# Turning the rows of 36 time steps by DMA over 16-bit planes instead of on TensorE, and loading the first weight block in quarters

## The chip, the core and the metric

One core of a Trainium2 chip runs the whole program. It has five engines that each work through their own instructions in order: TensorE (PE, with its weight load PEld), VectorE (DVE), ScalarE (ACT), GpSimd (POOL) and SyncE (SP, which only issues transfers here). An instruction that waits for a semaphore holds everything behind it on its engine. The metric is the device time of one execution in microseconds (us), lower is better.

## What is computed

The input `x` is 128 rows (b) x 64 time steps (t) x 512 values, so 8192 tokens. A GRU (hidden size 512) runs over the 64 steps; its output goes through a linear layer with ternary weights and is added to `x`. Then a causal convolution along b and a mixture of experts follow, whose sum with `x` is the output. Cut to what matters here:

```
x = x + ffn0(gru(cond_2048, x))            # 64 steps, one after the other
c = conv(x, cond_2048)                     # tokens that the second half works on
y = moe(c): softmax(c @ gate_w.T), top 6 of 64 experts, SwiGLU of each (512 -> 352 -> 512)
shared = silu(c @ sw_gate) * (c @ sw_up) @ sw_down        # 512 -> 704 -> 512, all tokens
out = x + y + shared
```

All matrix products are 32-bit floats.

## The kernel before

The program has four stages, and TensorE is at work in all of them: the GRU (0 to about 1150 us), the convolution (to about 1280 us), the shared experts with the routing (to about 1765 us), and the routed experts, with the rest of the shared ones between them (to the end).

**The first stage's start.** `load_xt(0, ...)` brings the first step's input, and `load_halves` (L295) each input weight block of 1 MB in two transfers of 512 KB, all on SP's queue. TensorE multiplies the raw weights at once (`products`, L336), and DVE and ACT cut each 128 x 512 part into a high, a low and a mixed part (`convert`, L356 to L366).

**The convolution's result** lies in two tiles, `hid0` and `hid1`, of 128 partitions (b) x 32 steps x 512 values; `hid(t)` is one step's 128 x 512 values (2 KB in each partition, 256 KB in all).

**The third stage** has 16 groups of NB = 4 steps; `rows_of(i)` are the steps 4i to 4i + 3. The loop over `i` in 0..7 does in each iteration:

- `shared(i)`: the shared experts of group i. Five blocks (`Block`) of seven products each (`winograd`, L824: two fp32 products of 256 columns), then two times seven for the way back (`Down`). Products 1, 6, 7, 3 (of the block before), 2, 4, 5 write into the PSUM banks `psx`, `y`, `psw`, `psz`. Product 1 is copied out of `psx` by ACT (L853), product 2 is then added onto the same bank, and ACT's silu (L864) reads it; only after that may the next block's product 1 write `psx`. DVE does the sums (L855, L858, L867, L860, L861, L870, L871). `shared` is a generator: it yields 44 times.
- `route` of the groups 2i + 1 and 2i + 2, some pieces of it at each yield of `shared`. Each of their 8 steps has to be turned first, so that the 512 values lie across partitions: `turn(t)` (L1120) makes four TensorE transposes of 128 x 128 (L1128) into a PSUM bank, and DVE copies the bank back over `hid(t)` (L1138). For steps from 32 on the turned rows are also stored to `xts` in HBM by SP (L1144), since a later stage reads them. Then come the gate products (`lg`, L1152), softmax, top 6 and counts; SP stores the scores (L1196).
- `add_shared(i)`: POOL issues four transfers that add group i's result, which stands in `rows_of(i)` by then, to the output in HBM (L1106).

Iteration i also uses `rows_of(i - 2)` as scratch space for its sums (`sums_space`), from i = 2 on. Before the loop `put_rows` stores the unturned rows to `tab`, all through SP's queue.

The order on each engine is set by a scheduler that takes the instructions in the order written, but moves an instruction forward where its own estimate says that the engine would be free and the operands ready. What stands in an engine's list is then done strictly in that order.

Of the kernel before, what the change touches and what calls it, by code (L numbers as in the profile page):

```python
# [9 lines left out]
BF16 = mybir.dt.bfloat16  # L10
I32 = mybir.dt.int32
U8 = mybir.dt.uint8
F32R = mybir.dt.float32r
AF = mybir.ActivationFunctionType
ALU = mybir.AluOpType
# [4 lines left out]
P = 128  # L20
B = 128
T = 64
D = 512
KD = D // P
# [23 lines left out]
def adaln_ffn_kernel(  # L48
# [22 lines left out]
    nc = tc.nc  # L71
# [10 lines left out]
    xts = dram.tile([T // 2, P, D], F32, name="xts")  # L82
# [10 lines left out]
        out=before,  # L93
        in_=before,
# [11 lines left out]
    def load_rows(dst, src):  # L106

        return nc.sync.dma_start(out=dst, in_=src.rearrange("(k p) n -> p k n", p=P))
# [98 lines left out]
    HK = KD // 2  # L207
    HD = D // 2
    gis_ = ExitStack()
    ps_gi = gis_.enter_context(tc.tile_pool(name="ps_gi", bufs=1, space=PSUM))  # L210
    with (
# [19 lines left out]
        def planes(pool, name):  # L231
            return [pool.tile([P, KD, D], F32R, name=f"{name}{n}") for n in "hls"]

# [7 lines left out]
        raw_i = [st.tile([P, KD, D], F32, name=f"rawi{c}") for c in range(3)]  # L241
# [9 lines left out]
        cols = [slice(c * D, (c + 1) * D) for c in range(3)]  # L251
        xps, xns, parts_of = {}, {}, {}

        def load_xt(t, queue=nc.gpsimd):
            xps[t] = xpp.tile([P, KD, B], F32, name="xp")
            queue.dma_start(out=xps[t], in_=xT[t])
# [34 lines left out]
        def repeated(dst, row):  # L291
            nc.sync.dma_start(out=dst, in_=row.partition_broadcast(P))

        def load_halves(dst, src):
            for k in range(2):  # L295
                load_rows(dst[:, k * HK : (k + 1) * HK], src[k * HD : (k + 1) * HD])

        h = el0.tile([P, D], F32, name="h")
        bh = {0: io0.tile([P, D], F32, name="xn"), 1: el0.tile([P, D], F32, name="n")}

        load_xt(0, nc.sync)
        load_halves(raw_i[0], w_ih[:, cols[0]])
        load_halves(raw_i[2], w_ih[:, cols[2]])
        nc.sync.dma_start(out=h, in_=cond)
        load_xt(1, nc.sync)
        load_halves(raw_i[1], w_ih[:, cols[1]])
        load_rows(raw_h[0], w_hh[:, cols[0]])
        repeated(br, b_ih[cols[0]])
        repeated(bh[0], b_hh[cols[0]])
# [20 lines left out]
        def banks(c):  # L330
            pool = ps_gh if c == 1 else ps_gi
            return [pool.tile([P, D], F32, name=n) for n in BANKS[c]]
# [37 lines left out]
        def split_x(t):  # L370

            xp = xps.pop(t)
            cut = xpp.tile([P, KD, B], F32, name="xcut", bufs=1)
            parts_of[t] = [el0.tile([P, KD, B], F32R, name=f"x{n}") for n in "hls"]
            xh, xl, xs = parts_of[t]
# [46 lines left out]
        def place(t, n):  # L422

            if t < T - TAIL:
                return xpp.tile([P, KD, B], F32R, name=f"h{n}", bufs=1)
            return el0.tile([P, KD, B], F32R, name=f"x{n}")

# [52 lines left out]
        def cell_r(t, ps):  # L480
            a, b = ps
            r = el0.tile([P, D], F32, name="rz")
            if t == 0:
                nc.vector.tensor_add(r, b, br)
            else:
                nc.vector.scalar_tensor_tensor(r, a, WHOLE, br, ALU.mult, ALU.add)
                nc.vector.tensor_add(r, b, r)  # L487
            nc.scalar.activation(r, r, AF.Sigmoid)  # L488
            return r

        def cell_n(t, ps, r):
            a, b = ps
            n = el0.tile([P, D], F32, name="n")
            if a is None:
                nc.vector.tensor_add(n, b, bhn)
            else:
                nc.vector.scalar_tensor_tensor(n, a, WHOLE, bhn, ALU.mult, ALU.add)
                nc.vector.tensor_add(n, b, n)
            nc.vector.tensor_mul(n, n, r)
            nc.vector.tensor_add(n, n, gis.pop((t, 2)))  # L500
            nc.scalar.activation(n, n, AF.Tanh)  # L501
            nc.vector.tensor_sub(h, h, n)
            return n
# [15 lines left out]
        for c in (0, 2, 1):  # L519
            a, b = banks(c)  # L520
# [14 lines left out]
        r = cell_r(0, first[0])  # L535
        n = cell_n(0, (None, first[2][1]), r)
# [41 lines left out]
        for t in range(1, T):  # L578
# [17 lines left out]
            r = cell_r(t, ps_r)  # L596
            n = cell_n(t, ps_n, r)
# [11 lines left out]
            if t in (1, 2):  # L609
# [9 lines left out]
                else:  # L619
                    sgn = wh0.enter_context(  # L620
                        tc.tile_pool(name="sgn", bufs=1, reuse_waits="tile")
                    ).tile([P, KD, D], F32R, name="sgn")
                    wf = wi.tile([P, KD, D], F32, name="q")
# [37 lines left out]
    TH = T // 2  # L661


    cum = ctx.enter_context(tc.tile_pool(name="cum", bufs=1)).tile([P, T, NE], U8, name="cum")
    first = ExitStack()
# [9 lines left out]
    def hid(t):  # L675
        return hids[t // TH][:, t % TH, :]
# [21 lines left out]
    with tc.tile_pool(name="ps_c", bufs=4, space=PSUM) as ps_c:  # L698
        for sl in range(NSL):
# [6 lines left out]
            for g in range(DS // 4):  # L706
# [4 lines left out]
                d = slice(g * 4, g * 4 + 4)  # L711
# [9 lines left out]
            if sl >= TAIL_AT:  # L721
# [3 lines left out]
                d = slice(0 if sl == TAIL_AT else 2 * DS * sl, 2 * DS * (sl + 1))  # L725
# [3 lines left out]
            for n in range(2):  # L729
                if sl == NSL - 2 + n:  # L730
                    d = slice(2 * DS * sl, 2 * DS * (sl + 1))
# [61 lines left out]
    NB = 4  # L793
# [3 lines left out]
    def behind(instructions, when=True):  # L797
        return tc.issue_after(instructions[-1].ins) if when and instructions else nullcontext()
    NI = T // NB
# [304 lines left out]
    def add_shared(i):  # L1104
        for t in range(i * NB, i * NB + NB):
            nc.gpsimd.dma_start(out=out_t[t], in_=rows_of(i)[:, t % NB], accum_op=ALU.add)  # L1106


    with (
# [10 lines left out]
        def turn(t):  # L1120

            if t in (2, 3):
                ps = ps_y.tile([P, D], F32, name="y")
            else:
                ps = ps_t1.tile([P, D], F32, name="pst1")
            ps = ps.rearrange("p (k b) -> p k b", k=KD)
            for k in range(KD):
                last = nc.tensor.transpose(ps[:, k, :], hid(t)[:, k * P : (k + 1) * P], ident)  # L1128
            return ps, last

        def route(its, turned={}):


            for i in its:
                for t in range(i * NB, i * NB + NB):
                    ps = turned[t] if t in turned else turn(t)[0]
                    with behind(marks, t in turned):
                        copied = nc.vector.tensor_copy(  # L1138
                            hid(t).rearrange("p (k b) -> p k b", k=KD), ps
                        )  # L1140
                    if t == NB - 1:
                        marks.append(copied)
                    if t >= TH:
                        nc.sync.dma_start(out=xts[t - TH], in_=hid(t))  # L1144
                    yield
# [21 lines left out]
            for n, i in enumerate(its):  # L1167
# [27 lines left out]
                for a in range(2):  # L1195
                    nc.sync.dma_start(  # L1196
                        out=tab_t[i * NB + 2 * a : i * NB + 2 * a + 2, :, D:].rearrange(
                            "t b e -> b t e"
                        ),
                        in_=sc[:, a::2, :NE],  # L1200
# [7 lines left out]
                for j in range(NB):  # L1208
                    t, r = i * NB + j, 2 * (j % 2) + j // 2
# [17 lines left out]
        def put_rows(i):  # L1227
            if i < NI:

                with tc.issue_after(loaded.ins):  # L1230
                    for t in range(i * NB, i * NB + NB):
                        (nc.gpsimd if i == 1 else nc.sync).dma_start(
                            out=tab_t[t, :, :D], in_=hid(t)
                        )
# [5 lines left out]
        for j in range(2):  # L1240
            nc.sync.dma_start(out=swdr[j * rest : (j + 1) * rest, :], in_=sw_down[full * P :, :])

        ahead = route([0])
        for _ in range(NB):
            next(ahead)
# [8 lines left out]
        for i in range(NI // 2):  # L1254
            put_rows(2 * i + 3)
            put_rows(2 * i + 4)

            def routing():
                if i == 0:
                    yield from ahead  # L1260
                its = [r for r in (2 * i + 1, 2 * i + 2) if r < NI]
                yield from route(its, second if i == 0 else {})

            routing_ = routing()
            done = 0
            for n, _ in enumerate(shared(i)):
                if done * PIECES <= n * 20:
                    with behind(products or marks, i == 0):
                        next(routing_, None)
                    done += 1  # L1270
            for _ in routing_:
                pass
            add_shared(i)
    first.close()
# [324 lines left out]
    for i in range(NI // 2 + 1, NI):  # L1599
        n = i - NI // 2 - 1  # L1600
        sums = None
        if i == NI - 1:
# [3 lines left out]
                out=sums, in_=out_t[i * NB : (i + 1) * NB].rearrange("t b d -> b t d")  # L1606
# [58 lines left out]
```

## Time and profile before

| | us |
|---|---|
| three runs | 2452.25, 2450.68, 2452.76 (median 2452.25) |
| the profiled execution: its own time | 2452.42 |
| its span, first to last instruction | 2450.7 |
| one iteration of the third stage's loop (i = 2 to 6) | 59.5 |
| DVE / ACT / POOL busy in one such iteration (i = 3) | 37.6 / 14.4 / 3.5 |

The profile is of one execution. A chain of waits follows the work that ended last back to the start; a group's row gives how often an instruction ran and for how long; a timeline row gives start, duration, engine, line and, in brackets, how long the engine was idle before and what ended that. Matmuls overlap, so their durations in a timeline add up to more than the time they take; the chain gives the time that each adds. The granted TensorE clock is 0.999 of full speed over the span.

### The profile page before, as it was taken

What the parts mean: (1) busy time and instruction counts of PE and PEld (TensorE: products, weight loads), DVE (VectorE), ACT (ScalarE), POOL (GpSimd) and SP (SyncE); (2) the same over time, 40 slices, a digit from 0 to 9 for tenths busy, and PEclk for the clock granted to TensorE, in tenths of its full rate; (3) what the DMA queues carried; (4) which work ended last, traced back from release to release, by engine and by line L of the source; (5) the groups of instructions that cost most, each with busy time, mean ns of one, the idle gap of its engine ahead of it and who ended that gap; (6) DMA issues with size and microseconds to landing.
All of it is one profiled execution on the core that took longest, in us unless ns stands there. A gap on an engine that the chain in (4) does not pass through costs nothing.

```text
span 2450.7 us, 32124 instructions
## 1 busy us (share of the span) xinstructions
PE 2436.9 (99%) x12317; PEld 1883.7 (77%) x12317; DVE 1546.5 (63%) x3073; ACT 463.1 (19%) x847; POOL 445.8 (18%) x468
## 2 busy tenths in 40 slices
PE   9999999999999999999999999999999999999999
PEld 5888888888888888888896688888876666666667
DVE  8877777777777776777686566666653433343344
ACT  5211111111111111111122222222211111111111
POOL 1122221122112112211220000000012222222220
PEclk9999999999999999999999999999999999999999
DMA  5244443333232223222497112222468999899962
GB/s 183 68 95 81 82 80 63 61 69 65 56 61 56 56 56 62 56 52 52 142 343 270 24 23 44 62 59 61 116 174 287 300 290 312 267 330 293 283 175 52
DMA packets 464456, 322.33 MB, mean 132 GB/s; under 512 B 316592, under 2 KB 384176, under 8 KB 462128
## 3 DMA queue, kind: packets, MB, share of 16 engines
q1 hardware_dynamic: 435408, 246.34, 35.6%
q0 software_dynamic: 28896, 73.95, 13.5%
q8 instruction: 97, 1.59, 0.3%
q14 instruction: 55, 0.45, 0.1%
HBM read 233.44 MB, written 92.03 MB: 133 GB/s over the span
## 4 chain that ended last, share of the span: by engine, by line
PE 98%; DMA 1%; DVE 0%; issue 0%; ACT 0%; SPq 0%; POOL 0%; DVEq 0%; ACTq 0%
PE psa L336 9%; PE psx L336 9%; PE psw L336 9%; PE psx L824 8%; PE psw L824 8%; PE psz L824 8%; PE psy L336 5%; PE psb L336 5%; PE psz L336 5%; PE psf L336 5%; PE y L824 4%; PE py L1550 3%; PE pg L1524 3%; PE pu L1524 3%; PE y L1001 2%; PE psc L193 2%
## 5 line engine op out<-in xcount | busy, mean ns | idle before, releaser
L1534 DVE SCALAR_TENSOR_TENSOR a<-a,rw,pu 128x352 f32<-128x352 f32 x32 | 18.6, 580 | 213.4 <-PE pu L1524 213.4
L354 DVE SCALAR_TENSOR_TENSOR xs<-xl,xcut 128x512 fp32r<-128x512 f32 x63 | 103.6, 1644 | 66.0 <-POOL xl L353 66.0
L347 DVE TENSOR_SCALAR hcut<-pst 128x512 int32<-128x512 int32 x63 | 43.5, 691 | 129.8 <-PE pst L419 127.6
L1106 POOL DMA_DIRECT2D out_dram<-hid x32 | 27.7, 1006 | 449.6 <-issue 333.5
L353 POOL TENSOR_TENSOR xl<-xp,xcut 128x512 fp32r<-128x512 f32 x60 | 82.8, 1380 | 145.2 <-PE psa L336 145.1
L488 ACT ACTIVATE rz<-rz 128x512 f32<-128x512 f32 x64 | 40.5, 633 | 336.1 <-DVE rz L487 336.1
L433 ACT CAST hh<-hcut 128x512 fp32r<-128x512 f32 x61 | 37.9, 622 | 325.0 <-DVE hcut L347 325.0
L271 POOL DMA_DIRECT2D q<-in_x_dram x36 | 19.3, 537 | 409.7 <-DMA out_dram<-q 313.4
L1550 PE MATMUL py<-wd,aeT 128*64 128x512 f32 (+1 forms) x384 | 88.8, 597 | 0.0
L1524 PE MATMUL pg<-wg,xeT 128*64 128x352 f32 x512 | 81.2, 459 | 0.0
L1524 PE MATMUL pu<-wu,xeT 128*64 128x352 f32 x512 | 81.2, 459 | 0.0
L1561 POOL DMA_INDIRECT out_dram<-ys,idxp x32 | 47.0, 1469 | 183.4 <-DMA out_dram<-ys,idxo 103.7
L1561 POOL DMA_INDIRECT out_dram<-ys,idxo x32 | 45.0, 1407 | 174.3 <-DMA out_dram<-ys,idxp 168.1
L336 PE MATMUL psa<-wih1h,xh 128*128 128x512 f32 x252 | 74.5, 416 | 0.0
L271 POOL DMA_DIRECT2D xn<-in_x_dram x28 | 15.0, 536 | 319.1 <-DMA out_dram<-xn 258.3
L1524 PEld LDWEIGHTS pg<-wg,xeT 128*64 128x64 f32 x512 | 36.3, 136 | 47.4 <-issue 47.4
L864 ACT ACTIVATE g<-psx 128x256 f32<-128x256 f32 x80 | 30.7, 384 | 217.5 <-DVE aT L871 158.5
L501 ACT ACTIVATE n<-n 128x512 f32<-128x512 f32 x64 | 40.5, 633 | 163.3 <-DVE n L500 160.9
L336 PE MATMUL psw<-wih2h,xh 128*128 128x512 f32 x252 | 68.7, 394 | 0.0
L336 PE MATMUL psw<-wih2l,xl 128*128 128x512 f32 x252 | 68.5, 392 | 0.0
L336 PE MATMUL psa<-wih1l,xl 128*128 128x512 f32 x252 | 68.2, 392 | 0.0
L336 PE MATMUL psb<-wih1s,xs 128*128 128x512 f32 x252 | 68.1, 392 | 0.0
(429 smaller groups left out, 6170.2 us busy)
## 6 DMA issues: line engine op xcount, KB each, us to landing
wg<-in_w_gate_dram SPq DMA_DIRECT2D x64, 704.0 KB, 12.5
wu<-in_w_up_dram SPq DMA_DIRECT2D x64, 704.0 KB, 12.8
wd<-in_w_down_dram SPq DMA_DIRECT2D x64, 512.0 KB, 10.5
xc<-x1c SPq DMA_DIRECT2D x32, 512.0 KB, 6.8
xp<-in_xT_dram POOLq DMA_DIRECT2D x62, 256.0 KB, 2.9
tab<-hid SPq DMA_DIRECT2D x56, 256.0 KB, 4.3
wd<-in_w_down_dram SPq DMA_DIRECT2D x64, 192.0 KB, 10.7
q<-in_x_dram POOLq DMA_DIRECT2D x36, 256.0 KB, 2.9
```

Source lines behind the costliest of these rows:

```text
L193: i = nc.tensor.matmul(ps[rows, j].rearrange("p h (u t) -> p h u t", u=2), xcs[sl % NCB][:, rows, g * 4 + j], tzs[sl % NCB][:, :, :, g * 4 ...
L336: i = nc.tensor.matmul(ps, lhs[:, k, :], rhs[:, k, :], start=start and k == 0, stop=stop and k == KD - 1, skip_group_check=True,)
L347: return nc.vector.tensor_scalar(dst.bitcast(I32), src.bitcast(I32), LOW, None, ALU.bitwise_and)
L353: i = engine.tensor_sub(lo, full, cut)
L354: nc.vector.scalar_tensor_tensor(mix, lo.bitcast(F32), -SPLIT, cut, ALU.mult, ALU.add)
L488: nc.scalar.activation(r, r, AF.Sigmoid)
L501: nc.scalar.activation(n, n, AF.Tanh)
L824: i = nc.tensor.matmul(ps.rearrange("p (j b) -> p j b", b=P) if len(r.shape) == 3 else ps, lhs(k), r, start=(first and k == 0), stop=(k == ...
L1001: nc.tensor.matmul(gu.rearrange("p (j b) -> p j b", b=P), swr[:, k].rearrange("p w n -> p (w n)"), rows[:, k], start=(k == 0), stop=(k == ...
L1524: nc.tensor.matmul(acc[halves[j]], self.xeT[:, k, halves[j]], self.ws[j][which][:, k, :], start=(k == 0), stop=(k == KD - 1),)
L1550: nc.tensor.matmul(py[halves[j]], self.aeT[:n, c, halves[j]], self.ws[j][2][:n, c, :], start=(c == 0), stop=(c == len(ech) - 1),)
L1561: nc.gpsimd.indirect_dma_start(out=out, out_offset=bass.IndirectOffsetOnAxis(ap=(idxp[:CAP] if j == 0 else idxo)[:, q : q + 1], axis=0), i ...
```

## The change

Two edits, both in how data is moved:

1. Steps from 28 on (groups 7 to 15, 36 steps) are no longer turned on TensorE. `turn_away(i)`, run beside iteration i from i = 2 on, turns the groups 2i + 3 and 2i + 4, which are routed in iteration i + 1. For each step ACT copies the low and the high 16-bit halves of the 512 words into two planes of 512 half-words (`flat_at`, two buffers in turn), one SP transfer turns the 128 x 1024 half-words (`dma_start_transpose`, into `turned_at`, three buffers in turn), and two steps later DVE copies the two turned planes back as the halves of the words of `hid(t)`. The buffers are rows of `hid` that are done with: for i = 2 the rows 4, 5 and 6, 7, 3; after that 0, 1 and 2, 3, 7. `route` leaves out its turning loop, with its eight yields, from i = 3 on.
2. At the start the first input weight block comes in four transfers of 256 KB instead of two of 512 KB, and the first step's input is issued by ACT instead of SP. The other blocks stay in halves.

```diff
-        def load_halves(dst, src):
-            for k in range(2):
-                load_rows(dst[:, k * HK : (k + 1) * HK], src[k * HD : (k + 1) * HD])
+        def load_parts(dst, src, n=2):
+            for k in range(n):
+                load_rows(
+                    dst[:, k * KD // n : (k + 1) * KD // n], src[k * D // n : (k + 1) * D // n]
+                )
...
-        load_xt(0, nc.sync)
-        load_halves(raw_i[0], w_ih[:, cols[0]])
+        load_xt(0, nc.scalar)
+        load_parts(raw_i[0], w_ih[:, cols[0]], KD)
...
+        AWAY = 2
+        LAG = 2
+        def plane(t, n):
+            return hid(t).bitcast(U16)[:, n * D : (n + 1) * D]
+        def word_halves(t):
+            return hid(t).bitcast(U16).rearrange("p (d h) -> p d h", h=2)
+        def turn_away(i):
+            steps = [
+                t for r in (2 * i + 3, 2 * i + 4) if r < NI for t in range(r * NB, r * NB + NB)
+            ]
+            flat_at, turned_at = ((4, 5), (6, 7, 3)) if i == AWAY else ((0, 1), (2, 3, 7))
+            for n in range(len(steps) + LAG if steps else 0):
+                for w in range(2) if n < len(steps) else ():
+                    at = flat_at[n % 2]
+                    nc.scalar.copy(plane(at, w), word_halves(steps[n])[:, :, w])
+                    if w:
+                        nc.sync.dma_start_transpose(
+                            out=hid(turned_at[n % 3]).bitcast(U16).rearrange(
+                                "p (m b) -> p m b", b=P
+                            ),
+                            in_=hid(at).bitcast(U16),
+                        )
+                    yield
+                for w in range(2) if n >= LAG else ():
+                    t, at = steps[n - LAG], turned_at[(n - LAG) % 3]
+                    nc.vector.tensor_copy(word_halves(t)[:, :, w], plane(at, w))
+                    if w and t >= TH:
+                        nc.sync.dma_start(out=xts[t - TH], in_=hid(t))
+                    yield
...
-            for i in its:
+            for i in its if its[0] <= 2 * AWAY + 2 else ():
...
+            turning = turn_away(i) if i >= AWAY else iter(())
             for n, _ in enumerate(shared(i)):
                 if done * PIECES <= n * 20:
                     with behind(products or marks, i == 0):
                         next(routing_, None)
                     done += 1
+                next(turning, None)
             for _ in routing_:
                 pass
+            for _ in turning:
+                pass
             add_shared(i)
```

More of the change, by code (lines that the diff above doesn't have):

```diff
@@ L12 @@
 U8 = mybir.dt.uint8
+U16 = mybir.dt.uint16
 F32R = mybir.dt.float32r
@@ L292, in repeated @@
             nc.sync.dma_start(out=dst, in_=row.partition_broadcast(P))
-        def load_halves(dst, src):
-            for k in range(2):
-                load_rows(dst[:, k * HK : (k + 1) * HK], src[k * HD : (k + 1) * HD])
+        def load_parts(dst, src, n=2):
[3 more added lines that the diff above has]
+                )
         h = el0.tile([P, D], F32, name="h")
         bh = {0: io0.tile([P, D], F32, name="xn"), 1: el0.tile([P, D], F32, name="n")}
-        load_xt(0, nc.sync)
-        load_halves(raw_i[0], w_ih[:, cols[0]])
-        load_halves(raw_i[2], w_ih[:, cols[2]])
+        load_xt(0, nc.scalar)
+        load_parts(raw_i[0], w_ih[:, cols[0]], KD)
+        load_parts(raw_i[2], w_ih[:, cols[2]])
         nc.sync.dma_start(out=h, in_=cond)
         load_xt(1, nc.sync)
-        load_halves(raw_i[1], w_ih[:, cols[1]])
+        load_parts(raw_i[1], w_ih[:, cols[1]])
         load_rows(raw_h[0], w_hh[:, cols[0]])
```

## The prediction

> **What bounds the kernel now.** I first read the page's engine shares and the chain of work that ended last.
>
> ```profile
> PE 2436.9 (99%) x12317; PEld 1883.7 (77%) x12317; DVE 1546.5 (63%) x3073; ACT 463.1 (19%) x847; POOL 445.8 (18%) x468
> ...
> PE 98%; DMA 1%; DVE 0%; issue 0%; ACT 0%; SPq 0%; POOL 0%; DVEq 0%; ACTq 0%
> ```
>
> TensorE sets the end nearly everywhere, so work taken from it counts in full, as long as nothing else makes it wait. Next the chain in order of time, inside iteration 3 of the third stage:
>
> ```profile
> 1473.35 0.86 PE psw L824 x4
> 1474.21 0.44 PE pst L1128 x4
> 1474.65 0.86 PE psx L824 x4
> ...
> 1482.01 0.86 PE psx L824 x4
> 1482.88 0.44 PE pst L1128 x4
> 1483.31 0.86 PE psw L824 x4
> ```
>
> There is no gap: each product of two 256-column matmuls takes 0.86, and one step's four transposes take 0.44 between them. Busy times of this whole iteration (columns: stretch, length, PE, PEld, DVE, ACT, POOL, clock, share of the DMA engines, GB/s) show room on all other engines:
>
> ```profile
> 1467.55:1527.05 59.50, 59.50 (x306) 48.44 (x305) 37.56 (x114) 14.37 (x28) 3.46 (x4) 1.00 0.21 41
> ```
>
> For transfers I read the 256 KB rows of the same iteration (median us to landing):
>
> ```profile
> out_dram<-hid POOLq DMA_DIRECT2D x5, 256.0 KB, 5.6
> xts<-hid SPq DMA_DIRECT2D x4, 256.0 KB, 2.0
> ```
>
> The first quick one is a plain SP transfer, the other POOL's adding one. Then the timeline around the start of iteration 2, where the change begins:
>
> ```profile
> 1408.96 1.73 POOL L1106 DMA_DIRECT2D out_dram<-hid  x2 [8.11 <-ACT hid L1076]
> ...
> 1416.11 0.38 ACT L864 ACTIVATE g<-psx 128x256 f32<-128x256 f32 x1 [2.72 <-PE psx L824]
> ...
> 1423.55 0.39 ACT L864 ACTIVATE g<-psx 128x256 f32<-128x256 f32 x1 [4.10 <-DVE aT L871]
> ```
>
> Last the start of the kernel:
>
> ```profile
> 1.26 3.99 DMA rawi<-in_w_ih_dram
> ...
> 5.27 0.76 DVE L347 TENSOR_SCALAR cut<-rawi 128x512 int32<-128x512 int32 x2 [4.20 <-DMA rawi<-in_w_ih_dram]
> ```
>
> DVE first waits for half a weight block; from 5.27 to 40.53, when the first state is ready, it is busy 33.6 of 35.3 us, so DVE sets the pace there.
>
> **Transposes off TensorE: -15.7.** 36 steps x 0.435 (0.44 in the chain, 0.43 to 0.44 by the starts). TensorE's other work keeps its order, except that the gate products come earlier in an iteration. Iterations 3 to 6 shrink by 8 x 0.435 = 3.5 to 56.0, and iteration 7 by 1.7. It is worth the whole only if the products then follow without a gap. Already now, where nothing is left to turn (1438 to 1442), they follow at 0.86.
>
> **The start: -0.8.** The first quarter takes the place of the step's input on SP (issue at 0.81 instead of 1.26), and its 256 KB is half of what had to land. A 256 KB transfer in this trace lands after 2.0 at best, so at 2.8 at the earliest; at worst it lands like the half block, 3.99 after 0.81, at 4.8. DVE thus starts 0.45 to 2.4 earlier, but two issues more and one fewer on SP (0.5 each by its 1.97 for four) push the later blocks back 0.5, and the scheduler regroups the conversions. I take 0.8, bounds +1.0 and -1.5.
>
> **The new work by engine, off the path.** ACT: 72 copies of 128 x 512. The nearest row is ACT's 128 x 512 copy (L1076), 0.59. In ACT's list the 72 stand between the end of iteration 1 and the last block of iteration 4, so about 24 per iteration: 24 x 0.59 + 14.4 = 28.6 of 56. DVE: 36 copies out of PSUM go (0.69 each), 72 half-word copies come. None is in the trace; one-input rows are 0.42 (L347, SBUF to SBUF) and 0.69 (L1138). As they write every second half-word I take 0.69: 37.6 - 5.5 + 24 x 0.69 = 48.7 of 56. Both fit, so their throughput costs nothing. That cover is gone when a DVE copy takes 1.0 (37.6 - 5.5 + 24c = 56).
>
> **The turning transfer.** Its time T, from issue to landing, decides the rest. The trace has none. Below: 2.0, the plain 256 KB of the same stage and queue. Above: 5.6, POOL's adding transfer. I take 2.9, next to the slowest of the 32 `xts` stores (3.0) and equal to the input loads of the first stage (2.9).
>
> [...]
>
> **Where T costs.** ACT has two flat buffers: copy pair n + 2 waits for transfer n, and it stands in ACT's list in front of the silus that free `psx`. Two steps thus take T + 1.25 (two copies at 0.6 and a hand-over). In iteration 2 the first turned buffers are rows 6 and 7, which POOL's add of iteration 1 must have read: issued at 1408.96, landed 4.9 later (that stretch's median), at 1413.9. SP holds the first transfer until then. In ACT's list the pairs of steps 30 to 35 stand before block 1's silu L864, which comes at 1423.55 now; block 2's first product starts at 1425.54. After the first transfer the pairs of steps 30, 32, 34 and 35 (1.25 each) and two more transfers follow one another, so the silu would end at 1413.9 + T + (2T + 5.0) + 0.8 (ACT's two own operations in between) + 0.4, so TensorE stalls 3T - 5.4: 0.6 at 2.0, **3.3** at 2.9, 7.5 at 4.3 (median of the crowded `tab` stores), 11.4 at 5.6. The stalls inside block 0 and of DVE, which waits for turned planes ahead of its sums, are contained in this lag rather than added.
>
> The other 28 steps stand in two clusters: nine between 1451.5 and 1475.6 (4.5 cycles, 5.3 each) and seventeen in about 46 us of iterations 3 and 4 (8.5 cycles, 5.4 each). They keep up while T + 1.25 is below 5.35, T below 4.1, and cost 13 us per us above it. SP adds head-of-line waits: score stores (L1196, landing 1.7) stand behind transfers that wait for ACT, and DVE's next softmax writes the same tile. I allow 2 for that and for DVE's waits, from 0 to 6.
>
> **Sum:** -15.7 - 0.8 + 3.3 + 2.0 = -11.2 against the profiled execution's 2452.4 (span 2450.7, 1.7 around it; the median of the runs is 2452.25): **2441.2**. Its own range: 2435.8 (-15.7 - 1.5 + 0.6) to 2448.0 (T = 4.3: -15.7 - 0.8 + 7.5 + 2.6 + 2.0).
>
> **Rivals.**
> - *Given back (same).* T of 4.1 to 4.6 leaves between -5 and 0, about 2450. Or the fourth stage takes the gain: DMA is at 9 tenths in several late slices, streaming expert weights. Against that, the chain has DMA at 1% and its weight loads are released by TensorE, so they move with it; were it so, 2452.
> - *ACT's list becomes the bound (slower).* Place: the copy pairs that wait for a turning transfer ahead of `psx`'s silus, iterations 2 to 4. Price at T = 5.6: 11.4 + 13 x 1.5 + 2.0 - 16.5 = +16.4, so 2469. It loses from T = 4.6 on (3T - 5.4 + 13(T - 4.1) + 2 = 16.5). For it: large transfers at the start land after 10, the adding one after up to 10.9, and no row shows a transfer that scatters half-words. Against: DMA engines are at 0.21 here.
> - *DVE becomes the bound (slower).* If a half-word copy takes 1.38, twice the PSUM row, DVE needs 37.6 - 5.5 + 33.1 = 65.2 per iteration against 56, three times +9.2: -11.2 + 27.6 = +16.4, 2469. It loses above about 1.14. For it: the first stage's L354 takes 1.64 on average for 128 x 512, and the profile doesn't say why. Against: all other full-size rows of DVE lie between 0.42 and 0.95.
>
> **Chances.** Forecast 0.56, given back 0.17, ACT's list 0.17, DVE 0.10. A difference under 0.2% (4.9 us; the three runs spread over 2.1) I call the same. Faster 0.56, same 0.17, slower 0.27. The range goes from 2435.5, the forecast's low end, to 2461, halfway into the slower cases, and leaves out about 0.2 of the chance.
>
> **What would show it.** 36 of the 64 steps are gone from the L1128 group, and iterations 5 and 6, with no turning left beside them, last 56.0. Iteration 2 lasts about 63 instead of 59.5, TensorE idle before `psx` behind ACT's silu, ACT idle before half-word copies behind the turning transfer. Transfers land near 2.9, DVE half-word copies take 0.42 to 0.69. The first DVE conversion starts near 4.4. Wrong would be: T above 4.6, iterations 3 and 4 longer than 59.5, half-word copies above 1.1, or a gap in the experts' stage that eats the 11 us.

## The result: slower by 8 us

The changed kernel takes 2460.1 us (median of 8 runs, 2458.1 to 2461.3) against 2451.8 for the kernel before (8 runs beside it, 2450.7 to 2452.8): ratio 1.0033, interval 1.0022 to 1.0044. Forecast was 2441.2. The profiled execution took 2460.3 with a span of 2458.6, 7.9 more than before.

The page's engine line and chain shares of the changed kernel:

```profile
PE 2430.6 (99%) x12173; PEld 1875.5 (76%) x12173; DVE 1545.1 (63%) x3109; ACT 501.7 (20%) x919; POOL 448.2 (18%) x468
...
PE 39%; DMA 2%; ACT 1%; DVE 0%; issue 0%; SPq 0%; DVEq 0%; ACTq 0%
```

The shares of the second line cover only the span from 1406.6 on: followed back from the end, the chain stops there, at an adding transfer of POOL. Over the whole span little shows: TensorE is still at 99%, with 144 matmuls less (36 steps of 4), and 6 us less busy though 15.7 us of work were taken off. That gap says that the remaining products ran slower somewhere. The stretches of iterations 2 to 5 of the third stage show where (columns: stretch, length, PE, PEld, DVE, ACT, POOL, clock, share of the DMA engines, GB/s):

```profile
1405.10:1471.70 66.60, 62.76 (x306) 50.30 (x304) 41.86 (x130) 26.04 (x49) 3.46 (x4) 0.95 0.44 87
1471.70:1537.60 65.90, 60.57 (x274) 47.34 (x272) 39.59 (x126) 24.57 (x48) 3.46 (x4) 0.92 0.46 92
1537.60:1603.80 66.20, 61.02 (x275) 46.83 (x273) 42.79 (x139) 29.68 (x58) 3.46 (x4) 0.95 0.70 152
1603.80:1659.80 56.00, 56.00 (x275) 45.42 (x273) 32.62 (x106) 14.45 (x29) 3.46 (x4) 1.00 0.16 24
```

All 36 turnings lie in the first three rows. Iteration 5, with none beside it, takes the 56.0 that all should. Iteration 2, which still turns eight steps on TensorE, has 59.5 us of work, iterations 3 and 4 have 56.0. So 27.2 us are lost: 14.35 with TensorE idle (length less PE) and 12.85 with it busy longer than its work, at a clock of 0.92 to 0.95. In these rows DVE has over 23 us to spare and ACT over 36: neither is short of throughput.

The chain in order of time passes from iteration 2 into iteration 3 without a product of TensorE for over 30 us:

```profile
1466.44 5.77 DMA hid<-hid
...
1472.23 1.14 ACT hid L1154 x2
1473.36 0.28 ACT hid L975
1473.64 1.13 SPq L1156
...
1474.87 7.64 DMA hid<-hid
...
1482.53 0.47 DVE hid L1165
...
1483.06 0.61 ACT hid L1154
...
1483.69 3.04 DMA hid<-hid
...
1486.83 0.47 DVE hid L1165
...
1487.34 0.61 ACT hid L1154
1487.95 0.26 ACT g L1200
1488.21 3.52 DMA hid<-hid
...
1491.81 0.62 ACT hid L1154
1492.43 0.28 ACT g L867
```

`DMA hid<-hid` is the turning transfer, L1154 ACT's copies into planes, L1165 DVE's copies back. Transfer, copy, transfer, copy follow one another, and what TensorE needs (the logits' copy L1200, the silu L867) stands behind them in ACT's list. POOL issues the adding transfers of iteration 2 in two pairs:

```profile
1464.56 1.73 POOL L1109 DMA_DIRECT2D out_dram<-hid  x2 [56.73 <-ACT u L924]
1474.19 1.73 POOL L1109 DMA_DIRECT2D out_dram<-hid  x2 [7.90 <-ACT hid L975]
```

These pairs land after 5.3 and 7.1 in the median. The two turning transfers that run beside them take 5.77 and 7.64, the later ones 3.04 and 3.52. What TensorE does at the start of iteration 2 and in this stretch (its timeline, in brackets the idle time before and what ended it), and two stretches of the clock:

```profile
1416.54 2.07 PE L827 MATMUL psw<-hid,st 128*128 128x256 f32 x4 [3.38 <-DVE u L861]
...
1479.92 1.03 PE L827 MATMUL y<-hid,st 128*128 128x256 f32 x4
1483.61 2.08 PE L827 MATMUL psw<-hid,sw1first 128*128 128x256 f32 x4 [2.67 <-DVE hid L1026]
1488.27 0.69 PE L1213 MATMUL pst<-ident,g 128*128 128x128 f32 x2 [2.58 <-ACT g L1200]
```

```profile
1485.00:1490.00 5.00, 2.42 (x7) 1.50 (x6) 1.66 (x5) 2.52 (x6) 0.00 (x0) 0.50 1.07 272
...
1495.00:1500.00 5.00, 5.00 (x25) 4.41 (x24) 4.82 (x27) 3.62 (x7) 0.00 (x0) 1.00 0.49 140
```

In iteration 2 it waits for DVE's sum L861, in iteration 3 first for DVE's sum L1026, which stands behind a half-word copy, then for ACT's copy L1200; between and after the waits products take up to 2.08 instead of 1.03, with the clock at 0.53 from 1415 to 1420 and at 0.50 from 1485 to 1490.

Over the run, the groups and issue rows (after the last bar: idle before, and what ended it):

```profile
L1154 ACT COPY hid<-hid 128x512 uint16<-128x512 uint16 x72 | 42.0, 616 | 58.7 <-DMA hid<-hid 53.3 <-DMA out_dram<-hid 4.8 <-PE y L827 0.4
...
L1165 DVE COPY hid<-hid 128x512 uint16<-128x512 uint16 x72 | 30.7, 452 | 35.1 <-DMA hid<-hid 35.0
```

```profile
hid<-hid SPq DMA_TRANSPOSE x36, 3.2
```

The transfers land after 3.0 at the least, 3.2 in the median, 7.6 at most. At the start DVE's first conversion comes at 4.75 instead of 5.27 and the third stage begins at 1282.1 instead of 1285.0.

### The profile page after: what moved, and what is told of

The parts are those of the page before. It is cut to its first block, busy times and chain, and to the rows that moved or that the text cites. A ratio compares the mean times of both kernels' runs of the same rounds, so it can differ in the third digit from the quotient of the medians.

```text
span 2458.6 us, 32041 instructions
## 1 busy us (share of the span) xinstructions
PE 2430.6 (99%) x12173; PEld 1875.5 (76%) x12173; DVE 1545.1 (63%) x3109; ACT 501.7 (20%) x919; POOL 448.2 (18%) x468
## 5 line engine op out<-in xcount | busy, mean ns | idle before, releaser
L350 DVE TENSOR_SCALAR hcut<-pst 128x512 int32<-128x512 int32 x63 | 43.5, 691 | 130.6 <-PE pst L422 128.4
L858 DVE TENSOR_TENSOR u<-u,y 128x256 f32<-128x256 f32 x80 | 33.5, 419 | 60.8 <-PE y L827 56.1
L867 ACT ACTIVATE g<-psx 128x256 f32<-128x256 f32 x80 | 30.6, 383 | 200.1 <-DVE aT L874 152.2
L339 PE MATMUL psy<-wih0s,xs 128*128 128x512 f32 x252 | 68.2, 392 | 1.0 <-DVE rz L487 1.0
```

Source lines behind the costliest of these rows:

```text
L339: i = nc.tensor.matmul(ps, lhs[:, k, :], rhs[:, k, :], start=start and k == 0, stop=stop and k == KD - 1, skip_group_check=True,)
L350: return nc.vector.tensor_scalar(dst.bitcast(I32), src.bitcast(I32), LOW, None, ALU.bitwise_and)
```

## The experiments

My theory after the result: a turning transfer is quick enough alone, but the scheduler pulled the copies forward from where they are written (eight steps in each iteration 2 to 5, four in 6) into iterations 2 to 4. There they wait for transfers in front of work that TensorE needs, beside POOL's adding transfers. Rivals: the copies' own work on ACT and DVE; the slowness of this kind of transfer; TensorE's clock as a cause of its own.

Lengths of the iterations 1 to 7 in the profile (us), the start of the third stage, and the time (median of n runs):

| kernel | start | 1 | 2 | 3 | 4 | 5 | 6 | 7 | time (n) |
|---|---|---|---|---|---|---|---|---|---|
| before | 1285.0 | 61.3 | 59.5 | 59.5 | 59.5 | 59.5 | 59.5 | 56.0 | 2451.8 (8) |
| changed | 1282.1 | 61.4 | 66.6 | 65.9 | 66.1 | 56.0 | 56.0 | 54.0 | 2460.1 (8) |
| e1_start_only | 1282.3 | 61.3 | 59.5 | 59.5 | 59.5 | 59.5 | 59.5 | 56.0 | 2449.4 (10) |
| e2_no_transfer | 1281.5 | 62.7 | 63.4 | 57.2 | 55.9 | 56.0 | 56.0 | 54.0 | 2439.1 (1) |
| e3_no_adds | 1280.7 | 61.5 | 63.6 | 60.3 | 63.2 | 56.0 | 56.0 | 54.0 | 2447.6 (1) |
| e10_plain | 1282.5 | 61.3 | 62.3 | 60.7 | 62.3 | 56.0 | 56.0 | 54.0 | 2447.7 (1) |
| e4_spread | 1282.0 | 61.9 | 60.6 | 56.5 | 56.5 | 56.7 | 56.3 | 54.0 | 2436.6 (4) |
| e5_act_held | 1280.7 | 61.1 | 62.6 | 58.1 | 58.3 | 59.3 | 57.9 | 54.0 | 2444.4 (1) |
| e6_dve_held | 1283.1 | 61.3 | 63.3 | 56.6 | 57.9 | 57.3 | 56.3 | 54.0 | 2442.1 (1) |
| e8_spread_twice | 1282.4 | 61.4 | 66.3 | 62.9 | 63.2 | 62.3 | 62.6 | 54.0 | 2467.5 (1) |
| e9_filled | 1281.7 | 61.6 | 70.3 | 68.8 | 69.5 | 56.0 | 56.0 | 54.0 | 2470.6 (4) |
| e12_fill_one | 1280.7 | 61.4 | 65.0 | 65.3 | 67.3 | 56.0 | 56.0 | 54.0 | 2458.9 (6) |
| e13_same_lists | 1282.5 | 61.3 | 65.4 | 66.2 | 66.6 | 56.0 | 56.0 | 54.0 | 2460.4 (6) |
| e7_from_group5 | 1283.0 | 61.5 | 56.5 | 56.5 | 57.8 | 56.5 | 56.3 | 54.0 | 2434.5 (4) |
| e11_later | 1282.2 | 61.5 | 57.6 | 56.7 | 57.1 | 56.7 | 56.8 | 54.0 | 2435.3 (4) |

**The start alone.** The kernel before with the second edit:

```diff
-        load_xt(0, nc.sync)
-        load_halves(raw_i[0], w_ih[:, cols[0]])
+        load_xt(0, nc.scalar)
+        load_parts(raw_i[0], w_ih[:, cols[0]], KD)
```

> The kernel before with the second edit alone: the first weight block in quarters, the first step's input issued by ACT. If the 2.9 us by which the third stage began earlier in the changed kernel come from this edit, the third stage starts near 1282.1 instead of 1285.0, its iterations keep 59.5, and the whole is 2449.0 (2448 to 2450). If they come from elsewhere, for instance from a shift of the scheduler's order, the time stays at 2451.8 and the stage starts at 1285.

The ratio to the kernel before is 0.9991 (0.9981 to 1.0001), 2.4 us at an interval that just reaches 1. The start of the third stage moves as expected, and the fourteen profiled kernels with this edit have it between 1280.7 and 1283.1. So the edit gains some two to three us, at the edge of what the runs can tell, and the loss is the other edit's alone.

**Without the transfer.**

```diff
-                    at = flat_at[n % 2]
+                    at = turned_at[n % 3]
...
-                    if w:
-                        nc.sync.dma_start_transpose(
...
```

> The changed kernel without the 36 turning transfers: ACT copies its two planes straight into the buffers from which VectorE copies them back, so the rows of the steps from 28 on stay unturned and the routing sees other values. All 72 ACT copies and 72 VectorE copies remain. If the waits for the transfers cost the 27 us in iterations 2 to 4, iteration 2 falls from 66.6 to about 59.5 and iterations 3 and 4 from 66 to 56 to 57, span about 2433. If it is the work of ACT and VectorE itself, iterations 3 and 4 stay above 60 and the span above 2445.

Iterations 3 and 4 fall to 57.2 and 55.9, as the theory says, and the time to 2439.1. But iterations 1 and 2 keep 1.4 and 3.9 too much, without any transfer to wait for: with the transfers gone the scheduler drew the copies still further forward (all into iterations 1 to 3), and crowded among sums and silus they cost 6.4 us in all. Most of the 27 is the waiting, a smaller part is the crowding by itself.

**Without POOL's adding transfers.**

```diff
-            add_shared(i)
+            if i not in (1, 2, 3, 4):
+                add_shared(i)
```

> The changed kernel without POOL's adding transfers of iterations 1 to 4, so the shared experts' result of these groups is missing from the output. If the turning transfers grow from 3.2 to between 5 and 7.6 us because they run beside the adding ones, and the first of them wait for rows that these read, the landings stay near 3.2 throughout, iterations 3 and 4 take 56 to 58, iteration 2 about 61 and the span is near 2437. If a turning transfer is slow by itself, or slowed by the stores beside it, iterations 2 to 4 stay between 64 and 67 and the span above 2455.

In between. In iterations 3 and 4, where ACT's and SP's lists stay those of the changed kernel and DVE's too but for one sum that trades places with a memset, 8.5 of the 20.0 us lost are gone, but 11.5 stay. The chain there:

```profile
1467.99 3.14 DMA hid<-hid
...
1472.58 4.12 DMA hid<-hid
...
1478.81 3.12 DMA hid<-hid
...
1488.46 3.05 DMA hid<-hid
...
1526.87 4.71 DMA hid<-hid
...
1534.33 3.15 DMA hid<-hid
```

Their stretches (columns as above):

```profile
1467.50:1527.80 60.30, 57.46 (x274) 44.99 (x272) 38.94 (x124) 23.94 (x47) 0.00 (x0) 1.00 0.38 83
1527.80:1591.00 63.20, 58.35 (x274) 44.73 (x272) 42.28 (x138) 28.87 (x57) 0.00 (x0) 1.00 0.64 139
```

No transfer in the chain of these two iterations is over 4.71, against 7.64 in the changed kernel, and the granted clock is 1.00. So the adding transfers do slow the turning ones, but transfers of 3 to 4.7 still lose in these lists.

**The copies kept where they are written.** Each copy gets an order edge behind the latest silu or copy of a block (ACT) or the latest sum (DVE):

```diff
+    acts, adds = [], []
...
-                nc.scalar.activation(self.g1, ps, AF.Silu)
+                acts.append(nc.scalar.activation(self.g1, ps, AF.Silu))
...
-                    nc.scalar.copy(plane(at, w), word_halves(steps[n])[:, :, w])
+                    with behind(acts):
+                        nc.scalar.copy(plane(at, w), word_halves(steps[n])[:, :, w])
...
-                    nc.vector.tensor_copy(word_halves(t)[:, :, w], plane(at, w))
+                    with behind(adds):
+                        nc.vector.tensor_copy(word_halves(t)[:, :, w], plane(at, w))
```

> The changed kernel with each ACT copy tied behind the latest silu or copy of a block, and each VectorE copy behind the latest sum, at the place where it is written: eight steps in each of iterations 2 to 5 and four in iteration 6, instead of all 36 in iterations 2 to 4. A step's plane is then some 10 us old before it is waited for. If the loss comes from the crowding, iterations 3 to 6 take 56 to 57, iteration 2 about 59.5 to 61, and the time is 2433 to 2437, faster than both kernels. If a turning transfer beside these blocks costs whatever its place, iterations 3 to 6 take over 59.5 and the time stays above 2450.

2436.6, ratio 0.9937 (0.9920 to 0.9953): faster than both kernels, with the same transfers, the same copies and the same adding transfers. The groups and the stretches of iterations 3 and 4:

```profile
L1158 ACT COPY hid<-hid 128x512 uint16<-128x512 uint16 x72 | 41.5, 614 | 5.5 <-DMA out_dram<-hid 3.9 <-DMA hid<-hid 1.5
...
L1170 DVE COPY hid<-hid 128x512 uint16<-128x512 uint16 x72 | 31.0, 449 | 0.0
```

```profile
1466.00:1522.50 56.50, 56.37 (x272) 45.41 (x270) 37.54 (x122) 22.57 (x45) 3.46 (x4) 1.00 0.47 98
1522.50:1579.00 56.50, 56.37 (x274) 45.42 (x272) 37.46 (x122) 22.56 (x45) 3.46 (x4) 1.00 0.47 98
```

The waits for transfers are gone: 53.3 to 1.5 on ACT, 35.0 to nothing on DVE. Where the copies stand in the lists was the cause.

**One engine held at a time.** The spread kernel without DVE's edges, then without ACT's:

```diff
-                    with behind(adds):
-                        nc.vector.tensor_copy(word_halves(t)[:, :, w], plane(at, w))
+                    nc.vector.tensor_copy(word_halves(t)[:, :, w], plane(at, w))
```

```diff
-                    with behind(acts):
-                        nc.scalar.copy(plane(at, w), word_halves(steps[n])[:, :, w])
+                    nc.scalar.copy(plane(at, w), word_halves(steps[n])[:, :, w])
```

> The spread kernel with only ACT's copies tied to their place; VectorE's copies go where the scheduler puts them. ACT's list is then as in the spread kernel (16 copies in each of iterations 2 to 5). If ACT's waits ahead of the silus are what held TensorE in the changed kernel, this stays at 2436 to 2439. If VectorE's waits ahead of its sums cost as much, the time is 2443 or more, with idle VectorE before its half-word copies.

> The spread kernel with only VectorE's copies tied to their place; ACT's copies go where the scheduler puts them: 22, 16, 16 and 14 in iterations 2 to 5 instead of 16 each. If ACT's early copies waiting for a flat buffer cost, iteration 2 and 3 lose 2 to 5 us each and the time is 2441 to 2448. If it is enough that VectorE does not wait, 2436 to 2439.

One run each: 7.8 and 5.5 us above the spread kernel. With DVE free its half-word copies wait 16.3 us for transfers and TensorE waits 5.2 for DVE's sum behind them; with ACT free its copies wait 43.5 and iteration 2 has 63.3. Either engine's waits cost, and with both free it is 23.5, more than the sum of the two. That is no clean sum: with DVE held, ACT's copies stand 22, 16, 16 and 14 in iterations 2 to 5, not where the changed kernel has them.

**Plain transfers in place of turning ones.**

```diff
-                        nc.sync.dma_start_transpose(
+                        nc.sync.dma_start(
...
```

> The changed kernel with a plain transfer of the 256 KB in place of each turning one, in the same place of every queue, so the rows of the steps from 28 on come back unturned and the routing sees other values. A plain transfer lands after about 2.0 to 2.3 instead of 3.2 to 7.6. If the waits are paid by the transfer's duration at an unchanged order, the loss lies between that of the kernel without a transfer and the changed kernel's: iterations 2 to 4 lose 10 to 15 us and the time is 2444 to 2449. If any transfer in these lists costs the same, it stays near 2458.

Iterations 2 to 4 lose 13.8 us, half of the changed kernel's, and the time is in the expected range. The order did not stay unchanged, as the expectation had it: the scheduler moved some copies. Between 1405 and 1604 the transfers from `hid` to `hid` are 14.0% of the chain, against 27.2% in the changed kernel, and over the run ACT's copies wait 34.7 us for them instead of 53.3. So this shows that a shorter transfer loses less, and that even a plain one loses in such lists; its size is no clean slope. The three longest in that stretch of the chain take 4.25, 5.32 and 4.05, from 1462.47, 1471.64 and 1528.23 on, near the borders of iterations 2, 3 and 4, where the changed kernel's turning ones take 5.77, 7.64 and 6.57 beside POOL's adding ones: landing late there is not particular to the turning kind.

**The transfer doubled in the spread kernel.**

```diff
-                    if w:
+                    for _ in range(2 * w):
                         nc.sync.dma_start_transpose(
```

> The spread kernel with each turning transfer issued twice into the same buffer, the second behind the landing of the first, so that a turned plane comes after about 6.4 us instead of 3.2. With the copies spread, two steps take about 10 us and a plane is waited for some 10 us after its issue, so the theory that the placing and not the duration of the transfer decides gives 2436 to 2440. If the 13 us per us above a duration of 4.1 from the prediction held here too, it would be 2436.6 + 13 x 2.3 = 2466.

2467.5 (one run): my theory's number was wrong by 30 us, and the 2466 from the prediction's rate came close. The copies wait again:

```profile
L1158 ACT COPY hid<-hid 128x512 uint16<-128x512 uint16 x72 | 41.3, 618 | 29.0 <-DMA hid<-hid 21.2 <-DMA out_dram<-hid 3.9 <-issue 3.2
...
L1170 DVE COPY hid<-hid 128x512 uint16<-128x512 uint16 x72 | 30.3, 451 | 23.8 <-DMA hid<-hid 23.7
```

I had taken 10 us for two steps from the way the code is written. In the spread kernel's own trace, from its third transfer of iteration 4 on, transfers are issued at 1538.6, 1540.6, 1544.1, 1547.2, 1551.0 and 1554.1, so two steps take 5.5 to 6.9. A doubled transfer, estimated at twice 3.2, so 6.4, with copies and a hand-over of 1.25 needs 7.7. That is 0.8 to 2.2 too long for each of 18 pairs of steps, an estimated 14 to 40 us, and the time rose by 30.9: with the copies evenly spread, a rate is a fair price. Placing decides, but with a margin of only 1 to 2.5 us over the 4.5 that T = 3.2 needs.

**Is it the clock?** First, matmuls that nobody reads in TensorE's long waits:

```diff
+    def fill(n):
+        ps = ps_gu.tile([P, D], F32, name="psz")[:, :QT]
+        with behind(products):
+            for _ in range(n):
+                last = nc.tensor.matmul(
+                    ps, ident, gw.rearrange("p k e -> p (k e)"), start=True, stop=True
+                )
+        return last
...
+                    fills = {(2, 4): 8, (3, 7): 6, (4, 7): 1}.get((i, n), 0) if c == 0 else 0
...
+                fills = {7: 6, 9: 8}.get(i, 0)
```

> The changed kernel with matmuls nobody reads put into TensorE's longest waits: eight of 256 columns (3.4 us) before the held product of iteration 2, six and six in iteration 3, one and eight in iteration 4, about 12.5 us of work in all where TensorE was idle for 14.4. If the drop of the granted clock after the idle stretches costs its own 12.9 us (TensorE's busy time in iterations 2 to 4 beyond 59.5, 56, 56), the clock stays at 1.00, the added work is free and the time falls to 2447 to 2450. If the clock is no cause of its own, the time stays at 2460 or rises by the part of the added work that no longer fits.

Slower than the changed kernel by 10.5. But this does not settle it: with the filling the scheduler orders ACT differently, and its list now has 5, 6 and 7 copies in a row ahead of a silu where the changed kernel has at most 4. So the next pair holds the copies of iteration 2 in the same places in both kernels, and only one has the eight matmuls in the first wait:

```diff
+        acts_at = {8: ("g1", 0), 9: ("g2", 0), 12: ("u2", 1), 14: ("g2", 1)}
...
+            due = [p for p in places if p <= n] if i == AWAY else []
+            tag = places[max(due)] if due else None
+            return behind([placed[tag]] if tag else [], tag)
...
+                    filled = [fill(8)] if (i, c, n) == (2, 0, 4) else []
```

> The changed kernel with eight matmuls of 256 columns that nobody reads (3.4 us) ahead of the one product of iteration 2 that waited 3.4 us and then ran at half clock, and with the copies of iteration 2 tied so that ACT's, VectorE's and SP's lists are exactly those of the next kernel, which lacks the eight. If the dropped clock is a cause of its own in iteration 2, TensorE stays at full clock there and iteration 2 is 2.5 to 3.5 us shorter than in the next kernel. If the transfers and the copies behind them set the pace, TensorE waits for them a little later instead and iteration 2 is as long, within 1 us, or longer.

> The kernel of the run before without its eight added matmuls: the changed kernel with the copies of iteration 2 tied to the same places, a few of them one or two operations later than in the changed kernel. Iteration 2 takes 63 to 67 us with a granted clock near 0.5 after its wait, the rest as in the changed kernel, 2456 to 2461. It is the yardstick for the run before; were iteration 2 at 60, the waits would be gone with the small shift and the pair would tell nothing of the clock.

The same two stretches at the start of iteration 2, first with the filling, then without:

```profile
1412.00:1417.00 5.00, 5.00 (x27) 4.39 (x26) 4.10 (x11) 2.60 (x6) 0.00 (x0) 1.00 0.58 111
1417.00:1422.00 5.00, 4.80 (x27) 3.92 (x25) 2.81 (x7) 2.97 (x7) 0.00 (x0) 1.00 0.53 94
```

```profile
1412.00:1417.00 5.00, 1.84 (x11) 1.30 (x10) 2.39 (x7) 2.38 (x5) 0.00 (x0) 1.00 0.66 116
1417.00:1422.00 5.00, 5.00 (x20) 4.16 (x21) 3.72 (x9) 2.89 (x7) 0.00 (x0) 0.66 0.64 118
```

The filling keeps the clock at 1.00 where it falls to 0.66 without, and in that stretch TensorE does 27 matmuls instead of 20. Yet iteration 2 takes 65.0 against 65.4, and the runs overlap (2458.0 to 2462.2 and 2458.6 to 2462.3, medians 1.5 apart). With the filling, block 1's first product starts 13.5 into the iteration instead of 15.1, and the gate products of iteration 2 start 27.4 into it instead of 27.8: the lead is used up waiting for ACT and DVE. In iteration 2 the dropped clock is a companion of the waits and costs about 0.4 us in this pair. For iterations 3 and 4 no such pair was run. There the chain, which has no product in it for 30 us, says the same, and the kernel without the adding transfers still loses 11.5 in them at a clock of 1.00.

**More turned, and later.** The spread kernel with the steps of groups 5 and 6 as well, turned beside iteration 1; then the same with the turning begun four places later in every iteration:

```diff
-        AWAY = 2
-        LAG = 2
+        AWAY = 1
...
-            flat_at, turned_at = ((4, 5), (6, 7, 3)) if i == AWAY else ((0, 1), (2, 3, 7))
+            flat_at, turned_at = {1: ((0, 1), (2, 3)), 2: ((4, 5), (6, 7, 3))}.get(
+                i, ((0, 1), (2, 3, 7))
+            )
+            LAG = len(turned_at) - 1
```

> The spread kernel turning eight steps more by DMA, those of groups 5 and 6, beside iteration 1, with two flat and two turned buffers there, so that VectorE's copy comes one step after its transfer, some 5 us, not two. If a plane that old has always landed, iteration 2 falls from 60.6 to about 57 and the time to 2433 (2432 to 2435). If transfers beside POOL's adding ones, up to 7.6 in the changed kernel, hold VectorE or ACT in iteration 1, this gives back 2 to 5 us and the time is 2435 to 2439.

```diff
-                next(turning, None)
+                if n >= 4:
+                    next(turning, None)
```

> The kernel that turns from group 5 on, spread, with the turning begun four places later in each iteration (about 5 us), after POOL's adding transfers of the iteration before have landed. If the 2.9 us of VectorE's remaining waits for a turned plane came from running beside these, iteration 3 goes from 57.8 to 56.5 and the time to 2433 (2432 to 2434.5). If the later end of an iteration's turnings makes the gate products at the start of the next wait, it rises to 2436 or more.

The first takes 2434.5, ratio 0.9927 (0.9910 to 0.9944), the fastest here: iteration 2 at 56.5 gains 4.1 over the spread kernel, and 2.9 us of waits for transfers come back on DVE, 1.3 in iteration 1 and 1.5 in iteration 4 (57.8; the expectation of the second kernel wrongly calls that iteration 3). Beginning later takes 0.7 off iteration 4 and adds 1.1 to iteration 2: 2435.3, no gain.

## Why the prediction was wrong

The forecast was 11 us faster, with a range of its own up to 2448.0; the kernel became 8 us slower. That 2460.1 still lies in the wide range is no merit of the forecast: its upper end, 2461, was stretched halfway into the slower rivals.

- **Transposes off TensorE, right in size.** Iterations 5 and 6 last 56.0 and iteration 7 54.0. The 15.7 are there to be had: the spread kernel gets 12.3 of them, after what its iterations 1 and 2 lose.
- **Start, right in sign, too small.** About -2.9 in the profile, forecast -0.8 with a bound of -1.5. DVE starts 0.5 earlier, and by 1285 the lead is 2.9; which of the regrouped conversions gives the rest was not traced.
- **Copies' cost, right.** DVE's half-word copy 0.45 (0.42 to 0.69 forecast), ACT's 0.62 (0.59). DVE is no bound.
- **T, right alone, wrong in company.** 3.2 in the median for 2.9, but 5.8, 7.6 and 6.6 at the borders of iterations 2, 3 and 4, beside POOL's adding transfers. I had that row only as an upper bound for T, not as a neighbour that makes it longer where it matters most. At best a turning transfer took 3.0, a plain `xts` store of 256 KB in the same kernel 2.0.
- **"They keep up while T + 1.25 is below 5.35": the step that failed.** It divided the length of a cluster by its number of cycles. In ACT's list six pairs of copies stand between the end of iteration 2's products and the first block's silu L867 in iteration 3. In the undisturbed iteration 5 that silu starts 11.2 us into the iteration and TensorE takes its bank again 1.5 later; but six pairs are three cycles, and two of the transfers in them took 5.8 and 7.6. The silu came at 1492.3, 20.6 us into the iteration. Slow transfers alone are not the reason: with none over 4.71 in the chain, iterations 3 and 4 still lost 11.5. An average over a cluster says nothing of the one instruction that is due first. I put -7.0 + 3.3 + 2.0 = -1.7 on iterations 2 to 4; they gave +20.1. (The count was short as well: nine and seventeen are 26 of the 28 steps.)
- **"DVE's waits are contained in this lag", and 2 us for the rest: failed too.** In iteration 2 TensorE's long wait (3.38) was not for ACT's silu but for DVE's sum L861 behind a half-word copy. With only ACT held, DVE's waits cost 7.8 us.
- **The rival "ACT's list becomes the bound"** was the right mechanism with the wrong threshold: I let it lose from T = 4.6 on; with these lists it loses at a median of 3.2.
- **"Spread over it"** in the change's own words was what the code writes and not what the lists hold: ACT's copies stand 4, 26, 18 and 24 in iterations 1 to 4. I had read that, and priced only the rate.

## What to carry to other kernels

When a transfer is put between two copies on in-order engines, find in each engine's list the first instruction that the busy engine needs behind the copy, and compare its due time with the landing, not the mean rate. Here the scheduler pulled the copies forward to where they block; an order edge to the place where they are written cost next to nothing and turned +8 us into -15. Price a transfer by the busiest moment it runs in, and look at how much margin is left.

## What was unexpected of the hardware

- A 256 KB turning transfer lands after 3.2 in the median, where a plain `xts` store takes 2.0 in the kernel before and 2.3 in the changed one, but beside POOL's adding transfers after up to 7.6. The DMA engines' share then reads 1.20 at only 126 GB/s (1475 to 1480), against 1.07 at 272 when the adding ones have landed (1485 to 1490). Plain ones in their place took up to 5.3 near the borders of iterations.
- In the changed kernel the granted clock read 0.53 (1415 to 1420) around a wait of 3.38 us and 1.00 from 1425 to 1435, and 0.50 (1485 to 1490) around waits of 2.67 and 2.58 and 1.00 from 1495 to 1505. In the pair of iteration 2 it fell to 0.66 after a wait of 3.16, and matmuls on unread data in that wait kept it at 1.00. That it cost only about 0.4 us in iteration 2, where it was tested, was the surprise: TensorE was ahead of the engines it waited for.
